# A graph kernel's gather buffers, handed out in pairs of quads instead of quad by quad

## The chip, the core and the metric

The kernel runs on one core of one Trainium2 chip. The metric is the device time of one execution in microseconds (us); where several executions were made, their median.

## What is computed

The reference is one message-passing layer of a graph network with a residual and a layer norm, in float32. There are N = 12500 nodes of D = 160 features (64 scalars and 32 vectors of 3) and E = 400000 edges, sorted by their destination `dst`.

```
h_s = s @ lin1_ws * a / sqrt(64);   h_v = v x lin1_wv * a / sqrt(32)        # per node
hid = silu(edge_scalars @ fc_w1 / 8);   w = hid @ fc_w2 / 8                  # per edge, 224 weights
es, ev = h_s[src], h_v[src]                                                  # a gathered row of 160 per edge
m_*   = products of the parts of w with es, ev and edge_attr (cross product included)
agg   = segment_sum(m_*, dst) / 4
o     = agg through lin2_ws, lin2_wv;   pre = sc + o;   gated = silu / sigmoid of pre
out   = layernorm(x + gated)
```

## The kernel before, in words

A first stage builds `h_tab`, the table of transformed nodes in DRAM (12500 rows of 160 floats, written by L350). It ends at about 60 us. All the rest is the edge stage, and the change lies in it.

**Tiles and quads.** A tile is 128 edges, one on each partition. There are 3125 tiles. `steps` (L131) groups them by four into 782 steps, here called quads 0 to 781 (the last has one tile). The loop at L814 walks through the quads. On each engine the instructions run in the order in which the loop writes them out (L807). Step n does this:

- `gather` (L450, called at L821): GpSimd issues one indirect DMA per tile (L454), four in a quad. Each fetches 128 rows of `h_tab`, chosen by the tile's `src`, into a quarter of a buffer `hg` of the pool `deep`, which has four such buffers (L656). Nothing else runs on GpSimd in this stage.
- `weights` (L467, TensorE): the 224 weights of every edge of the quad, into a PSUM buffer `pw`.
- `one_hot` (L530, VectorE): the edges' places in a window of 16 nodes, from `rel` and `iota`.
- `products` (L471, VectorE): one product at L477 and three at L485. They read `pw` and `hg` and write `pr`. The third L485 is the last reader of the quad's `hg`, and it is the one that raises VectorE's semaphore.
- `select_quad` (L539, VectorE): the one-hot rows times the edge attributes.
- `sum_up` for quad n-2 (L546, TensorE): the segment sums of the quad's four tiles, as matmuls into `pa`.
- In some steps more work is put in: `hidden` for every second quad (L445, L447), `close` (L735) and `turned` (L555 to L560) for finished blocks, `second` (L570, a burst of 22 matmuls) and `add` (L578), `finish` for finished nodes (L603 to L636), and `self_connection` (L715, L716).

**Waits.** An indirect gather waits on two things. It has one of eight DMA semaphores, used in turn, so it waits for the landing of the gather eight places before it. The first gather of a quad also waits on VectorE's semaphore, until the buffer's previous user is used up. With four buffers handed out in turn, the first gather of quad n waits for the third L485 of quad n-4. The first L477 of a quad waits for the landing of the quad's four gathers.

The loop at L885 redoes work for inputs whose destinations fall outside the windows; with these inputs its count is zero.

Of the kernel before, what the change touches and what calls it, by code (L numbers as in the profile page):

```python
# [10 lines left out]
F32 = mybir.dt.float32  # L11
# [9 lines left out]
P = 128  # L21
# [3 lines left out]
D = S + V3  # L25
# [6 lines left out]
Q = 4  # L32
# [21 lines left out]
def gnn_kernel(  # L54
# [104 lines left out]
    def index(t):  # L159
        a0, idx, _ = ahead(t)  # L160
        return idx[:, t - a0:t - a0 + 1]
# [62 lines left out]
    with tc.tile_pool(name="nodes", bufs=len(starts)) as nodes, tc.tile_pool(  # L224
        name="nodes_ps", bufs=6, space=PSUM
# [210 lines left out]
    def hidden(pool, psum, es, halves, t0, n):  # L436

        ph = psum.tile([2 * S, Q * P], F32, name="ph", tag="misc")
        hid = pool.tile([2 * S, Q * P], F32, name="hid")
        ends = [max(0, min(n, m - t0)) for m in halves]  # L440
        assert ends[0] >= ends[1]
        for k, c0, c1 in ((2 * S, 0, ends[1]), (S, ends[1], ends[0])):
            if c1 > c0:
                c = slice(c0 * P, c1 * P)
                nc.tensor.matmul(ph[:k, c], w1[:k, :k], es[:k, t0 * P + c0 * P:t0 * P + c1 * P],  # L445
                                 start=True, stop=True)
                nc.scalar.activation(hid[:k, c], ph[:k, c], AF.Silu, scale=1.0 / math.sqrt(64))  # L447
        return hid

    def gather(pool, idx):  # L450

        hg = pool.tile([P, Q, D], F32, name="hg")
        for t, i in enumerate(idx):
            nc.gpsimd.indirect_dma_start(  # L454
                out=hg[:, t, :], out_offset=None, in_=h_tab,
                in_offset=bass.IndirectOffsetOnAxis(ap=i, axis=0))
        return hg

    def weights(psum, hid, slots):

        pw = psum.tile([P, Q, 256], F32, name="pw")
        n = len(slots)
        for t in range(0, n, 2):
            half, c = slots[t]
            m = min(2, n - t)
            assert half == 0 and all(slots[t + k] == (k, c) for k in range(m))
            nc.tensor.matmul(pw[:, t:t + m, :NWT], hid[:m * S, c * P:(c + 1) * P], w2[:m * S, :m],  # L467
                             start=True, stop=True)
        return pw

    def products(pool, pw, hg, n, between=None):  # L471

        pr = pool.tile([P, Q, NPR], F32, name="pr", bufs=3)
        full = pr[:, :n, PIECE["w2a"] * V:]
        two = bass.AP(tensor=full.tensor, offset=full.offset,
                      ap=[full.ap[0], full.ap[1], [(PIECE["w1a"] - PIECE["w2a"]) * V, 2], [1, S]])
        nc.vector.tensor_mul(  # L477
            two,
            pw[:, :n, :2 * S].rearrange("p t (k c) -> p t k c", k=2),
            hg[:, :n, None, :S].to_broadcast([P, n, 2, S]))  # L480
        if between:
            between.pop(0)()
        for k, first in enumerate(("D0", "C0", "B0")):
            first = PIECE[first] * V
            nc.vector.tensor_mul(  # L485
                pr[:, :n, first:first + V3].rearrange("p t (i c) -> p t i c", i=3),
                pw[:, :n, None, 2 * S + k * V:2 * S + (k + 1) * V].to_broadcast([P, n, 3, V]),
                hg[:, :n, S:].rearrange("p t (i c) -> p t i c", i=3))
            if between:
                between.pop(0)()  # L490
        return pr
# [159 lines left out]
    with tc.tile_pool(  # L651
        name="fin", bufs=1
    ) as fin, tc.tile_pool(
        name="late", bufs=2
    ) as late, tc.tile_pool(name="edge", bufs=2) as edge, tc.tile_pool(
        name="deep", bufs=4  # L656
    ) as deep, tc.tile_pool(name="banks", bufs=1, space=PSUM) as banks:
        pw_ps = Banks(banks, "pw", Q * 256, 2)
        pa_ps = Banks(banks, "pa", 512, 2)
# [147 lines left out]
        with tc.manual_schedule(engines={ENG.PE, ENG.DVE, ENG.Activation, ENG.Pool}):  # L807
# [6 lines left out]
            for n, (c, i, tiles) in enumerate(steps):  # L814
# [6 lines left out]
                hg = gather(deep, [index(t) for t, _, _ in tiles])  # L821
# [63 lines left out]
        with tc.For_i(0, n_redo, 1):  # L885
            n_again = nc.values_load(again[0:1, 0:1], min_val=0, max_val=G)
            for half in range(2):
                nc.sync.dma_start(
                    bounds[:, :even].rearrange("o (c h k) -> o h c k", k=KB, h=2)[:, half],
                    in_pairs(rows[:, :even])[:, half])  # L890
            nc.sync.dma_start(bounds[:, even:], rows[:, even:])
            for t in range(BT):
                nc.sync.dma_start(of_tile[0].rearrange("(b t) -> b t", t=BT)[:, t:t + 1],
                                  bounds[0, :, None])
            with tc.For_i(0, n_again, 1) as g, tc.For_i(0, GT, 1) as k:
                t = g * GT + k
                idx = loads.tile([P, 1], I32, name="idx1", bufs=1)
                nc.sync.dma_start(idx, src[ds(g, 1), :, ds(k, 1)].rearrange("o p t -> p (o t)"))
                eat = loads.tile([P, 4], F32, name="eat1", bufs=1)
                nc.sync.dma_start(eat, ea[ds(g, 1), :, ds(k, 1)].rearrange("o p t k -> p (o t k)"))  # L900
                base0 = loads.tile([P, 1], I32, name="base1", bufs=1)
                nc.sync.dma_start(base0, of_tile[0:1, ds(t, 1)].to_broadcast([P, 1]))
                to = loads.tile([P, 1], I32, name="to1", bufs=1)
                nc.sync.dma_start(to, dst[:, ds(t, 1)])
                line = loads.tile([1, P], I32, name="line1", bufs=1)
                with nc.allow_non_contiguous_dma(reason="one tile's destinations"):
                    nc.sync.dma_start(line, dst[:, ds(t, 1)].rearrange("p o -> o p"))
                ends = loads.tile([1, 2], I32, name="ends1", bufs=1)
                for k, op in enumerate((OP.min, OP.max)):
                    nc.vector.tensor_reduce(ends[:, k:k + 1], line, AX.X, op)  # L910
                nc.sync.dma_start(least, ends[:, 0:1])
                low = loads.tile([P, 1], I32, name="low1", bufs=1)
                nc.sync.dma_start(low, least.to_broadcast([P, 1]))
                es = loads.tile([2 * S, SIDE * P], F32, name="es")
                nc.sync.dma_start(es[:S, :P], es_t[:, ds(t * P, P)])
                hid = hidden(edge, misc_ps, es, (1, 0), 0, 1)
                hg = gather(deep, [idx])
                pr = products(edge, weights(pw_ps, hid, [(0, 0)]), hg, 1)
                r = edge.tile([P, 1], F32, name="r", bufs=1)
                had = edge.tile([P, 2], F32, name="had", bufs=1)  # L920
                nc.vector.tensor_tensor(r, to, base0, op=OP.subtract)
                nc.vector.tensor_scalar(had[:, 0:1], r, 0.0, None, op0=OP.is_ge)
                nc.vector.tensor_scalar(had[:, 1:2], r, float(W), float(2 * NP), op0=OP.is_lt,
                                        op1=OP.mult)
                nc.vector.tensor_mul(had[:, 0:1], had[:, 0:1], had[:, 1:2])
                nc.vector.tensor_tensor(r, to, low, op=OP.subtract)
                nc.vector.tensor_add(r, r, had[:, 0:1])
                first = nc.values_load(ends[0:1, 0:1], min_val=0, max_val=N - 1)
                last = nc.values_load(ends[0:1, 1:2], min_val=0, max_val=N - 1)
                with tc.For_i(first, last + 1, W) as base:  # L930
                    base = nc.s_assert_within(
                        base, 0, N - 1, skip_runtime_bounds_check_because="it is at most `last`")
                    pa = pa_ps.tile([P, 512], F32, name="pa")
                    sel = select(late, r, eat)
                    add_tile(pa, 0, sel, 0, pr[:, 0], start=True, stop=True)
                    sa = late.tile([P, NPR], F32, name="sa")
                    nc.scalar.copy(sa[:ROWS], pa[:ROWS, :NPR])
                    tt = late.tile([P, 8, NO, W], F32, name="tt", bufs=1)
                    turned(misc_ps, sa, tt, 0, 1)
                    add(base, second(late, misc_ps, tt, 1), 0)  # L940
                    nc.vector.tensor_scalar_add(r, r, -float(W))
            for pool, job, most in [(fin, job, NF) for job in jobs] + [(fin, last_job, LAST)]:
                job_steps = finish(pool, misc_ps, *job, most=most)
                for f in job_steps[:job[1]]:
                    f()()
                for f in job_steps[job[1]:]:
                    f()
# [46 lines left out]
```

## Time and profile before

| what | value |
|---|---|
| median of 3 runs | 4008.95 us (4008.7 to 4012.74) |
| profiled execution, its own time | 4006.09 us |
| its span | 4004.3 us |
| mean granted TensorE clock | 0.968 |
| busy: TensorE / VectorE / ScalarE / GpSimd | 3666.2 / 2407.4 / 897.4 / 2973.4 us |
| the same as shares of the span | 92% / 60% / 22% / 74% |
| gathers L454: count, first and last start | 3125, 61.3 and 3971.1 us |

The profile is of one execution. [...] A group's line reads: line, engine, operation, out<-in, count | busy, mean ns of one | idle time of the engine just ahead of these instructions, and what ended most of it. "issue" means that the engine waited for nothing that the profile shows. The timeline lists instructions in order of time: start, duration, engine, line, and in brackets the idle time ahead. POOL is GpSimd, DVE is VectorE, ACT is ScalarE, PE is TensorE's matmuls and PEld its weight loads.

### The profile page before, as it was taken

The page shows a single profiled execution, that of the slowest core. Times are in us where ns is not written, and L with a number is a line of the kernel's source. Part 1 is how long each engine was busy: PE and PEld are TensorE (multiplying, and loading weights), DVE is VectorE, ACT ScalarE, POOL GpSimd, SP SyncE. Part 2 cuts the span into 40 slices and gives each one's busy share as a digit, 9 for nine tenths or more (in the row PEclk, how much of TensorE's full clock was granted, in tenths as well). Part 3 has the DMA queues.
Part 4 walks back from the last instruction along what each step waited for, and adds up shares of the span by engine and source line. Part 5 has one row for each costly group of instructions (what it writes and reads, how often), then busy time and mean ns, then how long its engine had stood idle before and what let it go on. Part 6 is the DMA issues. An engine that isn't in the chain of part 4 may idle for free. (4 is left out here: it accounts for less than half of the span.)

```text
span 4004.3 us, 46674 instructions
## 1 busy us (share of the span) xinstructions
PE 3666.2 (92%) x14291; PEld 1586.3 (40%) x14291; DVE 2407.4 (60%) x6508; ACT 897.4 (22%) x2488; POOL 2973.4 (74%) x3144
## 2 busy tenths in 40 slices
PE   6999899999989999999999899899898999989997
PEld 4344343443333433334334334344343433333343
DVE  5656565665665665656656556556565665665665
ACT  2222122221221221212212222122121221221222
POOL 4777777777777777777777777777777777777775
PEclk8999999999999999999999999999999999999998
DMA  8344344443443444444444444344344443443442
GB/s 243 95 100 101 95 106 98 105 101 95 105 102 95 106 102 95 103 99 101 102 99 102 98 103 104 95 106 102 95 106 98 104 100 95 109 99 96 102 98 54
DMA packets 227691, 411.71 MB, mean 103 GB/s; under 512 B 71883, under 2 KB 157383, under 8 KB 226535
## 3 DMA queue, kind: packets, MB, share of 16 engines
q0 software_dynamic: 152272, 266.53, 27.4%
q1 hardware_dynamic: 74646, 142.01, 14.6%
q8 instruction: 115, 1.88, 0.2%
q14 instruction: 144, 1.18, 0.1%
q10 hardware_dynamic: 514, 0.10, 0.0%
HBM read 392.41 MB, written 16.00 MB: 102 GB/s over the span
## 5 line engine op out<-in xcount | busy, mean ns | idle before, releaser
L454 POOL DMA_INDIRECT hg<-h_tab,idx x3125 | 2959.2, 947 | 958.2 <-issue 848.3
L467 PE MATMUL pw<-w,hid 128*128 128x448 f32 x3126 | 1370.6, 562 | 182.3 <-DVE sel L539 146.7
L546 PE MATMUL pa<-pr,sel 128*64 128x416 f32 x6250 | 1297.6, 537 | 0.0
L485 DVE TENSOR_TENSOR pr<-pw,hg 128x384 f32<-128x384 f32 x2346 | 1152.6, 546 | 0.0
L477 DVE TENSOR_TENSOR pr<-pw,hg 128x512 f32<-128x512 f32 x782 | 540.4, 691 | 992.3 <-DMA hg<-h_tab,idx 770.7
L467 PEld LDWEIGHTS pw<-w,hid 128*128 128x128 f32 x3126 | 555.9, 195 | 671.0 <-issue 453.2
L546 PEld LDWEIGHTS pa<-pr,sel 128*64 128x64 f32 x6250 | 386.2, 138 | 807.2 <-issue 797.1
L735 ACT COPY sa<-pa 128x416 f32<-128x416 f32 x521 | 263.2, 505 | 1259.4 <-PE pa L546 1257.2
L530 DVE TENSOR_TENSOR pw<-rel,iota 128x64 f32<-128x64 int16 x782 | 178.6, 228 | 500.6 <-PE pw L467 498.8
L445 PE MATMUL misc<-es,w 128*128 128x512 f32 (+1 forms) x784 | 452.7, 660 | 15.2 <-DMA es<-in_es_t_dram 13.5
L447 ACT ACTIVATE hid<-misc 128x512 f32<-128x512 f32 x392 | 233.5, 596 | 693.3 <-PE misc L445 693.0
L555 PEld LDWEIGHTS misc<-ident,sa 128*128 128x128 f32 x2084 | 240.3, 141 | 313.2 <-issue 265.6
L570 PE MATMUL misc<-tt,l 128*96 128x256 f32 (+5 forms) x1496 | 345.7, 378 | 4.6 <-DVE y L616 3.0
L555 PE MATMUL misc<-ident,sa 128*128 128x128 f32 x2084 | 328.6, 280 | 2.3 <-ACT hid L447 1.5
L539 DVE TENSOR_TENSOR sel<-pw,eas 128x256 f32<-128x256 f32 x782 | 321.8, 412 | 0.0
L570 PEld LDWEIGHTS misc<-tt,l 128*96 128x96 f32 (+1 forms) x1496 | 227.3, 163 | 143.3 <-issue 73.1
L558 ACT COPY tt<-misc 128x192 f32<-128x192 f32 x521 | 164.7, 316 | 505.5 <-PE misc L555 505.2
L445 PEld LDWEIGHTS misc<-es,w 128*128 128x128 f32 x784 | 120.1, 193 | 282.2 <-issue 224.7
L578 DVE TENSOR_TENSOR acc<-acc,os 96x32 f32 x1042 | 195.2, 187 | 25.2 <-ACT os L573 6.9
L603 PE MATMUL misc<-ident,acc 96*128 96x96 f32 x196 | 36.0, 269 | 95.4 <-DVE pw L530 46.2
L560 ACT COPY tt<-misc 128x64 f32<-128x64 f32 x521 | 117.1, 225 | 0.0
L573 ACT COPY os<-misc 96x512 f32<-96x512 f32 (+2 forms) x68 | 38.3, 563 | 296.4 <-PE misc L570 290.3
(83 smaller groups left out, 584.1 us busy)
## 6 DMA issues: line engine op xcount, KB each, us to landing
es<-in_es_t_dram SPq DMA_DIRECT2D x258, 384.0 KB
hg<-h_tab,idx POOLq DMA_INDIRECT x3125
h_tab<-ht POOLq DMA_DIRECT2D x6, 1280.0 KB
xt<-in_x_dram SPq DMA_DIRECT2D x23, 320.0 KB
out_dram<-y SPq DMA_DIRECT2D x23, 320.0 KB
xv<-in_xv_t_dram SPq DMA_DIRECT2D x25, 187.5 KB
xs<-in_xs_t_dram SPq DMA_DIRECT2D x25, 125.0 KB
xa<-in_xs_t_dram SPq DMA_DIRECT2D x6, 512.0 KB
```

The lines of the kernel that those rows point to most:

```text
L445: nc.tensor.matmul(ph[:k, c], w1[:k, :k], es[:k, t0 * P + c0 * P:t0 * P + c1 * P], start=True, stop=True)
L447: nc.scalar.activation(hid[:k, c], ph[:k, c], AF.Silu, scale=1.0 / math.sqrt(64))
L454: nc.gpsimd.indirect_dma_start(out=hg[:, t, :], out_offset=None, in_=h_tab, in_offset=bass.IndirectOffsetOnAxis(ap=i, axis=0))
L467: nc.tensor.matmul(pw[:, t:t + m, :NWT], hid[:m * S, c * P:(c + 1) * P], w2[:m * S, :m], start=True, stop=True)
L477: nc.vector.tensor_mul(two, pw[:, :n, :2 * S].rearrange("p t (k c) -> p t k c", k=2), hg[:, :n, None, :S].to_broadcast([P, n, 2, S]))
L485: nc.vector.tensor_mul(pr[:, :n, first:first + V3].rearrange("p t (i c) -> p t i c", i=3), pw[:, :n, None, 2 * S + k * V:2 * S + (k + 1) * ...
L539: nc.vector.tensor_mul(sel[:, :n], oh[:, :, None, :].to_broadcast([P, n, 4, W]), by_slot(tiles[0][0])[:, u:u + n, :, None].to_broadcast([P ...
L546: nc.tensor.matmul(pa[half * ROWS:(half + 1) * ROWS, :NPR], sel[:, t].rearrange("p k w -> p (k w)"), pr, start=start, stop=stop)
L555: nc.tensor.transpose(pt[:, four * P:four * P + k], sa[:k, c:c + P], ident[:k, :k])
L570: nc.tensor.matmul(po[:, k, :nb], l2[r, terms[to, part, four]], a[:, :nb], start=(n == 0), stop=(n == len(of) - 1))
L578: nc.vector.tensor_add(window, window, os[:, :, b])
L735: nc.scalar.copy(sa, pas.pop(j)[:, :NPR])
```

## The change

Instead of one buffer per quad, `gather` takes one tile of two quads from the pool and hands out its halves one after the other. The pool now has two such tiles, so the memory is the same: four quads of rows. A tile comes free as a whole. In the redo loop the list of halves is emptied ahead of the gather and after it.

```diff
+    pairs = []
+
     def gather(pool, idx):
 
-        hg = pool.tile([P, Q, D], F32, name="hg")
+        if not pairs:
+            both = pool.tile([P, 2, Q, D], F32, name="hg")
+            pairs.extend((both[:, 0], both[:, 1]))
+        hg = pairs.pop(0)
         for t, i in enumerate(idx):
             nc.gpsimd.indirect_dma_start(
...
-        name="deep", bufs=4
+        name="deep", bufs=2
...
+                pairs.clear()
                 hg = gather(deep, [idx])
+                pairs.clear()
```

In the instruction order of the two built programs, TensorE, VectorE, ScalarE and SyncE have the same instructions with waits on the same semaphores in the same places. On GpSimd the instructions are the same too; the waits on VectorE differ. Before, the first gather of every quad from quad 4 on has one. After, the first gather of every even quad from quad 4 on has one, and the odd quads have none. An even quad n opens the tile that held quads n-4 and n-3, so its wait is for the third L485 of quad n-3.

## The prediction

> **What bounds the kernel now.** I read the page's groups first, then the view of the tile `hg`, then the timeline of GpSimd and VectorE where they come closest. The groups:
>
> ```profile
> L454 POOL DMA_INDIRECT hg<-h_tab,idx x3125 | 2959.2, 947 | 958.2 <-issue 848.3
> ...
> L477 DVE TENSOR_TENSOR pr<-pw,hg 128x512 f32<-128x512 f32 x782 | 540.4, 691 | 992.3 <-DMA hg<-h_tab,idx 770.7
> ```
>
> GpSimd is busy 74%, TensorE 92%, so at first sight TensorE is the bound. The idle time says otherwise. GpSimd's 958.2 us over 3125 gathers is 0.307 us each, of which 848.3 us is "issue": a fixed gap behind every gather, not a wait. A gather takes 0.947 us and its gap 0.304, so one is issued each 1.251 us. The view of the tile has first and last start:
>
> ```profile
> L454 POOL DMA_INDIRECT hg<-h_tab,idx x3125: 942/946/1278, 61.3 to 3971.1; - x196
> ```
>
> 3124 x 1.251 = 3908 us, and 3971.1 - 61.3 = 3909.8. So **GpSimd's gathers run without one visible stall from end to end, and they bound the edge stage**. VectorE waits 770.7 us for their data. Before them lie 61 us of table building, behind them 3972.0 to 4004.3, the last sums and outputs. Any stall of GpSimd moves the end by as much, since nothing later catches up: TensorE and VectorE are ahead of their data and wait for it.
>
> **The change, step by step.** It adds and removes no instruction, no DMA and no byte: 3125 gathers as before, 4 quads of buffer as before. The order on PE, VectorE, ScalarE and SyncE is unchanged. What moves is one wait: the first gather of an even quad n waits for the third L485 of quad n-3 instead of n-4, and the odd quads' wait goes.
>
> *What the removed wait gives.* Nothing: it never holds. Over all quads from 4 on, the first gather starts 10.7 us (median) after the third L485 of quad n-4 ends, at the least 1.03 us (quad 4). Starts of first gathers of a quad follow their predecessor by 1.251 us, as the others do, so the wait costs no issue time either.
>
> *What the added wait costs.* I took from the timeline, for each of the 389 even quads from 4 to 780, the start of its first gather minus the end of the third L485 three quads earlier. This lead has a median of 5.5 us: GpSimd runs three quads (15.0 us) ahead, less 8.5 us from a quad's first gather to its last product. It is below 2 us in 33 places, below 1.03 in 16, below 0 in 6. The first is at the start, where VectorE still does setup when the gathers begin:
>
> ```profile
> 82.34 0.95 POOL L454 DMA_INDIRECT hg<-h_tab,idx  x1 [0.30 <-issue]
> ```
>
> ```profile
> 79.84 1.47 DVE L485 TENSOR_TENSOR pr<-pw,hg 128x384 f32<-128x384 f32 x3
> ...
> 82.43 1.47 DVE L485 TENSOR_TENSOR pr<-pw,hg 128x384 f32<-128x384 f32 x3
> ```
>
> The gather at 82.34 is the first of quad 4. It now waits for quad 0, done at 81.31; after the change for quad 1, done at 83.90: 1.57 us late. The largest one in the middle is quad 704:
>
> ```profile
> 3584.20 0.23 DVE L530 TENSOR_TENSOR pw<-rel,iota 128x64 f32<-128x64 int16 x1 [6.19 <-PE pw L467]
> 3584.47 0.69 DVE L477 TENSOR_TENSOR pr<-pw,hg 128x512 f32<-128x512 f32 x1
> 3585.08 1.47 DVE L485 TENSOR_TENSOR pr<-pw,hg 128x384 f32<-128x384 f32 x3
> ```
>
> ```profile
> 3584.43 0.94 POOL L454 DMA_INDIRECT hg<-h_tab,idx  x1 [0.30 <-issue]
> 3585.67 0.94 POOL L454 DMA_INDIRECT hg<-h_tab,idx  x1 [0.30 <-issue]
> ```
>
> VectorE sat idle for 6.19 us until TensorE gave it `pw`: TensorE did the burst of 22 matmuls of L570 and a slow stretch of L546 first. The products of quad 701 ended at 3586.55, the first gather of quad 704 started at 3585.67: 0.88 us late. Behind the waiting gather stand all later gathers, and the products wait for those.
>
> By place, the lateness (minus sign: lead left) is: quad 4 1.57, 32 -0.44, 128 0.08, 224 -0.25, 322 -0.35, 416 0.46, 476 0.00, 572 0.74, 608 -0.25, 704 0.88. Places close behind one of these (6 and 706, for example) are left out, as the stall gives them the same lead back. The rest have more than 0.87 left.
>
> *The price of a release.* A waiting gather doesn't start at the moment of the release; call the delay w. The trace shows no gather that waits for VectorE in earnest, so I bound it. Below: the six h_tab writes of L350 that wait for VectorE L339 start 0.29 to 0.31 us after its end, so w = 0.3. Above: quad 4's first gather started at its regular place with its release 1.03 us earlier, so w is at most 1.03. Nearest: the very first gather, the only one that found GpSimd idle, started at 61.27, after its last wait instruction ended at 60.47 (a record of the trace's semaphore events): w = 0.8. I take 0.8, as it is the same instruction; it may hold some start-up cost, which the range covers.
>
> The sum at w = 0.8: 2.37 + 0.36 + 0.88 + 0.55 + 0.45 + 1.26 + 0.80 + 1.54 + 0.55 + 1.68 = **10.4 us**. At w = 0.3 eight places are left and give 5.6 us; at w = 1.03 fourteen give 12.8. At w = 0 six give 3.7.
>
> [...]
>
> Against its own execution the sum is 4006.09 + 10.4 = 4016.5 us. The median of the runs shown is 2.9 us above that execution; the same 10.4 us on it give **4019.4 us**, which I forecast. No other cost: a stalled quad's data comes later, but VectorE is then behind by two quads whose data is there.
>
> **The rivals.**
>
> *Cheap release, no change that can be told (0.2%, 8.0 us, is about what a measurement of this kernel can tell).* If a blocked gather starts as promptly as the h_tab writes (w = 0.3), 5.6 us are left: 4014.5. The point from which it decides is w = 0.56, where the sum is 8.0. For it: six rows at 0.3, and the fixed gap between gathers is 0.304 too. Against: those are another kind of DMA, and the first gather took 0.8.
>
> *More stalls than this execution shows, slower.* Leads depend on when TensorE's bursts and late landings meet, which other executions may time otherwise. If every lead below 2 us became a stall at full price, the 33 places give up to 39 us (sum of 2 minus lead): 4048. For it: leads under 2 us are frequent. Against: the late places follow the written order, not chance: 32, 128, 224, 416, 608 and 704 lie multiples of 96 quads apart, and so do 476 and 572. I'd expect at most half, 4028.
>
> *The tile is tracked as a whole, so that the second quad of a pair waits for the products of the first.* Then GpSimd would stop at every odd quad for about 8.5 us minus 5.0, 390 x 3.5 = 1365 us: 5374. The instruction order has no wait on VectorE at odd quads, so this is nearly excluded.
>
> *Faster.* 389 waits go from GpSimd's order. If they cost anything, first gathers would follow later than the others; their mean distance is 1.2506 us against 1.2510 for the third of a quad. Nothing to win: 4009 at best.
>
> **How the numbers follow.** Forecast (w from 0.56 to 1.03, 4017 to 4022): 0.50. More stalls (4022 to 4048): 0.12. Cheap release, or stalls that other executions lack (4009 to 4017): 0.33. Whole-tile tracking: 0.01. Faster by over 0.2%: 0.04, for a cause that I don't see. So faster 0.04, same 0.33, slower 0.63. The range takes in the forecast, the lower end w = 0.3 (4014.5) less 2 us for fewer stalls, and half of the dense case: 4012.5 to 4028.
>
> **What would show it.** Right: GpSimd's groups keep 947 ns a gather, and its idle time grows by some 10 us, which the waits view puts on VectorE, L485 above all, in about ten places, quad 4 first with over 2 us; the last gather starts about 10 us later; VectorE's wait for gathers grows alike. Wrong if the gathers still run at 1.251 us throughout (the wait never bites), if the stalls sit at places with leads over 2 us, if a stall is much longer than its lateness plus 1 us, or if the mean gather or its gap changes.

## The result, and the profile after

The changed kernel takes **4017.59 us** in the median of 20 runs (4012.94 to 4028.3); the kernel before takes 4012.35 us in 20 runs beside it (4007.69 to 4020.15). The ratio is 1.0014, 95% interval 1.0008 to 1.0020, or 3 to 8 us. So the change costs some 5 us: clear of zero, and under the 0.2% (8 us) that the prediction called a difference.

The profiled execution has a span of 4020.5 us, 16.2 more than that of before. Most of this isn't the change. The view of the tile `hg` gives first and last start of the gathers (L459 is the old L454; from `gather` on, line numbers are 5 higher):

```profile
L459 POOL DMA_INDIRECT hg<-h_tab,idx x3125: 942/946/2334, 68.2 to 3985.2; - x196
```

The first gather starts 7.0 us later than in the profile of before. It waits for the whole of `h_tab`, and by the trace's semaphore events the last rows, which SyncE writes (L353), landed at 67.3 us instead of 60.3. Another profile of the same changed kernel starts at 61.3 (experiment 5). After the last gather 35.3 us follow instead of 33.2. Between first and last gather lie 3917.0 us instead of 3909.8: these 7.2 us are the part to explain. The page's groups:

```profile
L459 POOL DMA_INDIRECT hg<-h_tab,idx x3125 | 2961.0, 948 | 970.7 <-issue 901.8
...
L482 DVE TENSOR_TENSOR pr<-pw,hg 128x512 f32<-128x512 f32 x782 | 540.4, 691 | 1013.6 <-DMA hg<-h_tab,idx 808.5
```

A gather still takes 0.947 us and its gap 0.305. The gathers' own time is 1.8 us more; it differs by as much between executions (experiment 5 has 2958.5). VectorE's wait for gathers (808.5 instead of 770.7) differs between executions too: it is 762.1 in experiment 5, so it tells nothing of the change. The rest are waits. The view of GpSimd's waits (total, times, longest) now has VectorE's products with gaps over 0.3:

```profile
POOL hg L459 <- issue: 901.8, 2960, 0.3
...
POOL hg L459 <- DVE pr L490: 8.8, 12, 1.6
```

Of these 12, four are the usual gap, only named after VectorE. Eight are stalls; without the usual gap they are 0.87, 0.28, 0.79, 1.12, 0.03, 1.27, 0.16 and 0.64 us, **5.2 us in all**, at quads 92, 320, 322, 380, 382, 476, 572 and 704. All are first gathers of even quads. The longest is quad 476. The timeline of GpSimd there:

```profile
2455.03 0.95 POOL L459 DMA_INDIRECT hg<-h_tab,idx  x1 [0.30 <-issue]
2457.55 0.94 POOL L459 DMA_INDIRECT hg<-h_tab,idx  x1 [1.57 <-DVE pr L490]
2458.80 0.95 POOL L459 DMA_INDIRECT hg<-h_tab,idx  x1 [0.30 <-issue]
```

And of VectorE, which was using up quads 472 and 473:

```profile
2441.09 0.69 DVE L482 TENSOR_TENSOR pr<-pw,hg 128x512 f32<-128x512 f32 x1 [4.32 <-DMA hg<-h_tab,idx]
...
2453.78 0.26 DVE L535 TENSOR_TENSOR pw<-rel,iota 128x64 f32<-128x64 int16 x1 [5.98 <-PE pw L472]
...
2455.80 1.48 DVE L490 TENSOR_TENSOR pr<-pw,hg 128x384 f32<-128x384 f32 x3
```

Quad 473's last product ends at 2457.28 and the gather starts at 2457.55: **0.27 us after its release**. At all eight stalls the two starts and ends give 0.27.

Quad 476 also shows what lies ahead of a late product. TensorE's timeline and, below it, the busy times in three stretches (the column behind the five engines is TensorE's granted clock):

```profile
2438.64 1.67 PE L472 MATMUL pw<-w,hid 128*128 128x448 f32 x4
2442.78 0.55 PE L608 MATMUL misc<-ident,acc 96*128 96x96 f32 x2 [2.47 <-DVE y L621]
2443.26 2.83 PE L551 MATMUL pa<-pr,sel 128*64 128x416 f32 x8
2446.03 1.13 PE L445 MATMUL misc<-es,w 128*128 128x512 f32 x2
2446.99 5.25 PE L575 MATMUL misc<-tt,l 128*96 128x256 f32 x22
2452.08 1.67 PE L472 MATMUL pw<-w,hid 128*128 128x448 f32 x4
```

```profile
2432.00:2442.00 10.00, 7.67 (x32) 3.21 (x28) 4.30 (x12) 2.31 (x7) 7.56 (x9) 1.00 0.67 145
2442.00:2447.00 5.00, 4.22 (x13) 1.52 (x14) 4.86 (x14) 0.85 (x2) 3.78 (x5) 0.66 0.27 66
2447.00:2457.00 10.00, 10.00 (x44) 5.85 (x43) 3.65 (x11) 1.96 (x5) 6.84 (x8) 1.00 0.28 68
```

Read it from the top, as an order in time; that each step causes the next is not shown by it. A chunk of edge data is loaded (DMA share 0.67), a gather lands late, and VectorE waits 4.32 us for it. TensorE waits for VectorE and sits idle for 2.47 us. Towards the end of this its clock is halved for 3.4 us (by the trace's clock records from 2442.3 to 2445.8), and the eight L551 take 2.83 us instead of 1.62. The burst of 22 matmuls L575 follows, 5.25 us, and only behind it the weights `pw` that quad 473's products need. Each of the eight stalls has such a burst, or the end of one, in the 16 us ahead of it; of all even quads in this trace, 37% have one. Five of the eight have a half-clock stretch in the 18 us ahead; of all even quads, 22% have one.

### The profile page after: what moved, and what is told of

The parts are those of the page before. It is cut to its first block, busy times and chain, and to the rows that moved or that the text cites. A ratio compares the mean times of both kernels' runs of the same rounds, so it can differ in the third digit from the quotient of the medians.

```text
span 4020.5 us, 46285 instructions
## 1 busy us (share of the span) xinstructions
PE 3668.3 (91%) x14291; PEld 1584.5 (39%) x14291; DVE 2406.6 (60%) x6508; ACT 898.6 (22%) x2488; POOL 2975.3 (74%) x3144
## 5 line engine op out<-in xcount | busy, mean ns | idle before, releaser
L459 POOL DMA_INDIRECT hg<-h_tab,idx x3125 | 2961.0, 948 | 970.7 <-issue 901.8
L551 PE MATMUL pa<-pr,sel 128*64 128x416 f32 x6250 | 1300.4, 538 | 0.0
L482 DVE TENSOR_TENSOR pr<-pw,hg 128x512 f32<-128x512 f32 x782 | 540.4, 691 | 1013.6 <-DMA hg<-h_tab,idx 808.5
L551 PEld LDWEIGHTS pa<-pr,sel 128*64 128x64 f32 x6250 | 387.3, 139 | 811.1 <-issue 801.3
L535 DVE TENSOR_TENSOR pw<-rel,iota 128x64 f32<-128x64 int16 x782 | 178.8, 229 | 495.2 <-PE pw L472 493.2
L575 PE MATMUL misc<-tt,l 128*96 128x256 f32 (+5 forms) x1496 | 345.6, 378 | 7.6 <-DVE y L621 5.5
L575 PEld LDWEIGHTS misc<-tt,l 128*96 128x96 f32 (+1 forms) x1496 | 227.0, 162 | 144.6 <-issue 73.0
```

What stands on the lines that cost most here:

```text
L459: nc.gpsimd.indirect_dma_start(out=hg[:, t, :], out_offset=None, in_=h_tab, in_offset=bass.IndirectOffsetOnAxis(ap=i, axis=0))
L482: nc.vector.tensor_mul(two, pw[:, :n, :2 * S].rearrange("p t (k c) -> p t k c", k=2), hg[:, :n, None, :S].to_broadcast([P, n, 2, S]))
L551: nc.tensor.matmul(pa[half * ROWS:(half + 1) * ROWS, :NPR], sel[:, t].rearrange("p k w -> p (k w)"), pr, start=start, stop=stop)
L575: nc.tensor.matmul(po[:, k, :nb], l2[r, terms[to, part, four]], a[:, :nb], start=(n == 0), stop=(n == len(of) - 1))
```

## The experiments

**State of the theories.** *Stall theory*: the change costs the late places at pair openings, each its lateness plus a release price, and nothing else. *Pairing rival*: handing out in pairs costs something besides. Open beside these: what the price is, and what makes products late.

The first four kernels ran on another chip than the others, and there the kernel before took 5190.29 us instead of about 4010. I tell them after their repetitions.

**1. The change itself again** (experiment 5; no edit).

> The changed kernel itself, beside the kernel before. Where TensorE is granted a clock of about 0.97 (before near 4010 us), the stall theory has about eight stalls on VectorE L490, 4 to 7 us together, each starting 0.27 us after the release, and a ratio of 1.001 to 1.002; the quads that stall need not be the same ones. Where TensorE is granted about 0.87 (before near 5190 us, as on the chip of the first four experiments), gathers wait hundreds of times, and the pairing rival has the change 2% slower, since the moved pairs were 2.1% slower there; the stall theory in its first form, in which only the lead of three quads counts, has it like three single buffers, which were 0.4% faster there.

Measured: 4019.84 against 4015.74 us, ratio 1.0005 (0.9996 to 1.0014). The interval holds the first measurement's 1.0014, and also 1, no change. Its profile is clearer than its times. GpSimd's waits:

```profile
POOL hg L459 <- DVE pr L490: 8.1, 12, 2.8
```

There are seven stalls, 4.5 us in all: quad 4 with 2.53, and 128, 380, 382, 476, 572 and 704 with 0.02 to 0.78, each 0.27 us after its release. From first to last gather it is 3913.6 us. So quad 4 stalls when the gathers start early (61.3 us), and not when they start at 68.2; 380, 476, 572 and 704 come in both.

**2. More room: three tiles of two quads** (experiments 1 and 6).

```diff
-        name="deep", bufs=2
+        name="deep", bufs=3
```

> The change with three tiles of two quads again. At a clock of about 0.97: stall theory no gather waits for VectorE, ratio 1.000 within 0.001; pairing rival 1.0013. At about 0.87: 1.03 again, as in the first run of it.

Measured: 4015.48 against 4015.74 us, ratio 0.9997 (0.9988 to 1.0006). The view of GpSimd's waits has four entries for VectorE's products, all of them the usual gap:

```profile
POOL hg L459 <- DVE pr L490: 1.2, 4, 0.3
```

No stall; first to last gather 3909.7 us, as before (3909.8). Pairs as such cost nothing that can be told on this chip. The expectation for the same kernel on the other chip is told below.

**3. The pairs moved by one quad** (experiments 2 and 7).

```diff
             hide(0)
+            pairs.append(deep.tile([P, Q, D], F32, name="hg0", bufs=1))
```

> The pairs moved by one quad again. At a clock of about 0.97: stall theory at most two stalls near the start, up to 1 us, ratio 1.000 within 0.001; pairing rival 1.0013. At about 0.87: 1.02 again.

Measured: 4015.94 us, ratio 1.0001 (0.9992 to 1.0010). Two stalls, 0.33 us at quad 323 and 0.87 us at quad 609, 1.2 us in all; first to last gather 3910.6 us. The amount is as expected and the places aren't (not near the start). The output burst is always written into a step of the same parity, and the products behind it, of odd quads, are what an even quad's opening waits for. One quad further, a pair opens on the products behind those, and these are late less often: in the trace of before, eight even quads have a lead of under 0.27 us over the last product three quads back, and two odd ones (5 and 23).

**4. Three single buffers** (experiments 3 and 8): on the kernel before, `bufs=4` becomes `bufs=3`.

> Three buffers of one quad again. At a clock of about 0.97: stall theory the same stalls as the change and at most 1 us more, 4 to 7 us, ratio 1.001 to 1.002; pairing rival 1.000. At about 0.87: 0.996 again.

Measured: 4019.64 us, ratio 1.0008 (0.9999 to 1.0017), beside the change's 4019.84 in the same job. Five stalls, 5.4 us: quad 3 with 3.59 at the start, 23, 92, 476 and 704. So a lead of three quads stalls about as much with no pairs in it. The time alone doesn't show that: from first to last gather it is 3923.0 us, since a gather took 949 ns instead of 947, here and in experiment 3, which is 7 us over all of them. The reason is open.

**5. The same memory handed out in one piece** (experiment 10): tiles of four quads, one of them.

```diff
-            both = pool.tile([P, 2, Q, D], F32, name="hg")
-            pairs.extend((both[:, 0], both[:, 1]))
+            both = pool.tile([P, 4, Q, D], F32, name="hg")
+            pairs.extend(both[:, k] for k in range(4))
...
-        name="deep", bufs=2
+        name="deep", bufs=1
```

> The same memory handed out still more coarsely: one tile of four quads, whose first gather waits until all four are used up (the products of the quad just before). Stall theory: every fourth quad stalls, 195 stalls; a quad's products end 8.5 us after its first gather starts and the next quad would start 5.0 us after it, so each costs 3.5 + 0.27 us at least and more where products are late; by the trace of before 970 us, ratio 1.24 at a clock of 0.97. With a release price of 0.8 it would be 1070 us. If TensorE were the bound instead of GpSimd, the stalls would be covered and the ratio far smaller.

Measured: 4983.53 against 4008.80 us, ratio 1.2427 (1.2408 to 1.2446), 975 us more where 970 were expected. All 195 openings stall, 983 us together. Of GpSimd's timeline, one opening:

```profile
2007.14 0.95 POOL L459 DMA_INDIRECT hg<-h_tab,idx  x1 [0.30 <-DMA hg<-h_tab,idx]
2008.39 0.97 POOL L459 DMA_INDIRECT hg<-h_tab,idx  x1 [0.30 <-issue]
2014.77 0.94 POOL L459 DMA_INDIRECT hg<-h_tab,idx  x1 [5.41 <-DVE pr L490]
2016.02 0.95 POOL L459 DMA_INDIRECT hg<-h_tab,idx  x1 [0.30 <-issue]
```

191 of the stalled gathers start 0.27 us after the release and four 1.74 us after it. Stalls of GpSimd go nearly one to one into the time here: 983 us of stalls, 975 us of time. A plain sum over the leads in the trace of before, with 0.27 us for each release, gives 1040 us, so the leads size these stalls to some 6%.

**6. Two single buffers** (experiment 11): on the kernel before, `bufs=4` becomes `bufs=2`.

> The kernel before with two buffers of one quad: every quad waits for the products two quads earlier, half the memory. Stall theory: from the leads in the trace of before some 145 stalls, 230 us together, ratio 1.057 at a clock of 0.97, each stalled gather 0.27 us after its release. With a price of 0.8 it would be 295 us. If the change's cost came from the pairing and not from the lead, this kernel would be no slower than before by its stalls alone.

Measured: 4291.35 us, ratio 1.0696 (1.0680 to 1.0712), 283 us more. There are 202 stalls, 288 us together, more than the 145 and 230 expected, though 190 of them start 0.27 us after the release (12 after 1.74). The total lies near the one worked out with a price of 0.8, but that isn't its reason. The leads of before don't size this kernel well: where each stall moves all later gathers and products along, they give 223 stalls and 412 us, more than measured. TensorE idles more here (88% busy instead of 92%) and its granted clock is 0.952 instead of 0.968, so products are late at other places; how much that adds is not shown.

**7. The price that was put too high** (experiment 9): one more gather ahead of the first.

```diff
     nc.gpsimd.dma_start(dt, dst)
+    warm = consts.tile([P, D], F32, name="warm")
+    nc.gpsimd.indirect_dma_start(
+        out=warm, out_offset=None, in_=x,
+        in_offset=bass.IndirectOffsetOnAxis(ap=index(0), axis=0))
```

> The change with one more indirect gather, of 128 rows of x into a tile that nothing reads, on GpSimd ahead of the first gather of h_tab. It asks why the release price was put at 0.8 us: the first gather starts 0.80 us after its last wait instruction in every profile, a stalled gather 0.27 us after the product that releases it. If 0.8 is a cost of the first indirect gather of a program, the first gather of h_tab now starts about 0.3 us or less after its last wait instruction and the extra one takes the 0.8; if it belongs to a wait instruction ahead of any gather on an idle GpSimd, it stays at 0.8.

Measured, by GpSimd's timeline (in this kernel the gather is at L463):

```profile
56.31 1.04 POOL L359 DMA_INDIRECT warm<-in_x_dram,idx  x1 [0.30 <-issue]
62.15 0.97 POOL L463 DMA_INDIRECT hg<-h_tab,idx  x1 [4.80 <-DMA h_tab<-ht]
```

The last of the separate wait instructions ahead of the gather at 62.15 ended at 61.43 (by the trace's semaphore events), so it started 0.72 us behind it instead of 0.80. A first-time cost is at most 0.08 of it, and the 0.1 us by which the first gather is longer (1.04) moves to the extra one. Where the other 0.72 comes from is not shown. The first gather differs from a stalled one in two ways: it stands behind separate wait instructions, and all that it waits for are landings of DMAs, while a stalled gather carries its last wait itself, and that wait is for VectorE. No run here has one without the other.

The kernel's time in its one run was 4012.98 us, which tells nothing by itself. But its trace is a third profile of the change: nine first gathers stall, 4.4 us in all, at quads 4, 32, 188, 224, 322, 476, 572, 608 and 668, each 0.27 us after its release.

**8. Shorter bursts** (experiments 4 and 12): on the change, `NO = 16` becomes `NO = 8`.

> The change with NO = 8 again, bursts of half the columns twice as often. At a clock of about 0.97: stall theory fewer than three stalls on L490, under 1.5 us in all, not counting quad 4 at the start; TensorE's busy time grows by 50 to 100 us within its idle 330 us; ratio 0.999 to 1.001. Rival (late landings make products late): the same seven or eight stalls. A third way: more work on TensorE makes more products late and the stalls grow. At about 0.87: 1.02 again.

Measured: 4012.16 against 4008.80 us, ratio 1.0008 (0.9998 to 1.0017). There are nine stalls, 3.8 us in all, not fewer than three and under 1.5. On the page the bursts have 128 columns, and VectorE's products are still waited for (the next line is from the view of waits):

```profile
L575 PE MATMUL misc<-tt,l 128*96 128x128 f32 (+2 forms) x2926 | 385.7, 279 | 1.5 <-ACT tt L565 1.5
```

```profile
POOL hg L459 <- DVE pr L490: 5.9, 10, 1.0
```

The length of one burst isn't what decides. The stalls sit at other quads (56, 152, 442, 536, 698, 728 and so on), and seven of the nine have a half-clock stretch in the 18 us ahead, where 27% of the even quads have one. No quad 4 is among them (the gathers started at 65.5). My account of a burst as the cause was too simple: late products seem to need several things together, and a half-clock stretch is often among them. What makes products late stays open.

**9. The first four, on a chip where TensorE's granted clock was lower** (experiments 1 to 4). The expectations, in the order of the kernels above, three pairs, moved pairs, three singles, short bursts:

> The change with a third tile of two quads (six quads of rows instead of four), so the first gather of an even quad n waits for the products of quad n-5. Stall theory (the change costs only the late places at pair openings, each its lateness plus 0.27 us): no gather waits for VectorE, the idle time of the gathers falls by 5 us against the changed kernel, and the time is that of the kernel before, ratio 1.000 within 0.001. Rival (handing out in pairs costs something else: the start, longer gathers, a sequencer that runs less far ahead): still about 5 us slower than before, ratio 1.0013. If the release price were 0.8 us, the result here would be the same as by the stall theory.

> The change with the pairs moved by one quad: quad 0 has a buffer of its own, pairs are quads 1 and 2, 3 and 4, and so on, so that odd quads open the pairs and wait for the products three quads earlier. Stall theory: the late products are those of odd quads, behind a burst of 22 matmuls that is always written into a step of the same parity, and an odd quad waits for an even one. From the trace of before, two odd quads (5 and 23) have leads under 0.27 us, 1.0 us together, from the trace of the change none: 0 to 1 us of stalls, ratio 1.000 within 0.001. Rival (any pairing costs): 5 us, ratio 1.0013.

> The kernel before with three buffers of one quad instead of four: every quad waits for the products three quads earlier, the even ones as in the change. Stall theory: the change's stalls and at most 1 us more, 5 to 6 us, ratio 1.0013 to 1.0015, with the stalled quads almost all even. Rival (the cost lies in the pairing, not in the lead of three quads): as before, ratio 1.000.

> The change with NO = 8 instead of 16: the output step L575 comes twice as often, with 22 matmuls of half the columns. Stall theory: the burst of some 5 us gets shorter, so products behind it are less late; fewer than three stalls on VectorE L490, under 1.5 us in all, although TensorE gets more to do (some 60 more bursts; its busy time may grow by 50 to 100 us). The time goes back to about that of before, ratio 0.999 to 1.001, if TensorE's idle time covers its extra work. Rival (late products come from late landings of gathers, not from TensorE's burst): the same eight or so stalls, 5 us, or more.

Measured, against 5190.29 us before: three pairs 5367.46 (ratio 1.0315, 1.0284 to 1.0346), moved pairs 5305.22 (1.0211, 1.0178 to 1.0243), three singles 5167.19 (0.9961, 0.9936 to 0.9986), short bursts 5299.86 (1.0195, 1.0160 to 1.0230). Every expectation missed. The page of three pairs:

```profile
PEclk7888888888888888888888888888888888888898
...
L459 POOL DMA_INDIRECT hg<-h_tab,idx x3125 | 2956.2, 946 | 2312.3 <-DVE pr L490 1358.0
...
L535 DVE TENSOR_TENSOR pw<-rel,iota 128x64 f32<-128x64 int16 x782 | 182.7, 234 | 2638.1 <-remote 1231.1
```

TensorE's mean clock is 0.861 there (28% of the time at half), and VectorE is idle for 2638 us ahead of L535: 790 us of it ended by TensorE's `pw`, 1231 by something that the profile can't name. GpSimd, now no bound, waits 1358 us for VectorE even with six quads of room. So the stall theory's first condition, that the gathers bound the stage, is false on that chip, and its numbers don't apply. Whether the low clock is the cause is not shown: in experiment 10, on a chip that showed 0.97 with the kernel before, stalls left TensorE busy for 80% of the span instead of 92%, and the clock was 0.897. So a low clock goes with idle time there, and which comes first can't be told. There the three kernels that pair were 2 to 3% slower and three singles a little faster. The change itself wasn't run there. Why more room makes that chip slower is **open**.

## Why the prediction was right or wrong

*The gathers bound the stage: right on the chips of the result.* With no stall (three pairs) the time is that of before, and 983 us of stalls make 975 us of time. It was wrong on the chip of experiments 1 to 4, where the clock was 0.86.

*The removed wait gives nothing: right.* Three pairs have no effective wait on VectorE at all, and a ratio of 0.9997.

*The added wait bites at a few even quads, by the leads of before: right in kind and number.* Ten places were listed; eight stalls came in the first profile and seven in the second. Quads 322, 476, 572 and 704 (first) and 4, 128, 476, 572 and 704 (second) were on the list; 92, 320, 380 and 382 weren't, with leads over 0.9 us in the trace of before. In the first profile the listed places give 2.9 of the 5.2 us, and quad 4, which was to stall most, doesn't stall; in the second they give 4.3 of 4.5, in that of experiment 9 3.4 of 4.4. So the total agrees better than the places do, and in the first profile that is partly luck. The places recur at distances of 96 quads, as was said, but which of them are late differs by execution. Half-clock stretches are often near (five of the eight stalls in the first profile have one in the 18 us ahead). Of the 48 such stretches in the trace of before, 26 last 3.4 us and 20 last 6.8; in the 3.4 us ahead of one TensorE was idle for 2.7 us in the median. Why the places change from execution to execution is not shown by any run here.

*The price of a release: the step that failed.* The prediction bounded it by 0.3 and 1.03 and took 0.8, "the same instruction", from the first gather. It is 0.27 (all but a few, told below). The row that looked nearest was of the same instruction but of another wait (separate instructions, for landings), and its 0.8 doesn't carry over. The `h_tab` writes, the prediction's lower bound, are another operation, but they carry a wait for VectorE as a stalled gather does, and their 0.29 to 0.31 was close. With 0.27 the prediction's own list keeps eight places, 1.84 + 0.35 + 0.02 + 0.73 + 0.27 + 1.01 + 0.02 + 1.15 = 5.4 us, against 5.2 and 4.5 us of stalls in the two profiles and 5.2 us between the medians. The term was 10.4 us, twice too large. Nor is 1.03 a bound for every release: some took 1.74 us (experiments 10 to 12), though no first gather of a quad in the three profiles of the change. So the rival of the cheap release came, and the difference stays under 8 us, where "slower" had the larger chance.

*A length that was misread.* The prediction puts 8.5 us between a quad's first gather and its last product. That is near the shortest in the trace of before (8.4 us); the median is 9.4, which fits the median lead of 5.5 us (15.0 less 8.5 would be 6.5). The sum by places doesn't use it; the 1365 us of the whole-tile rival does, and is too small by it.

*The time.* 4019.4 was forecast and 4017.59 measured, and that they are only 1.8 us apart is luck: the term was some 5 us too large, and the median of before, 4012.35 over 20 runs, is 3.4 us above the one that I added to.

*More stalls than one execution shows: didn't come.* The sum stays at 4.4 to 5.2 us in the three profiles, although the places change.

## What to carry to other kernels

A buffer pool on a bounding engine can be priced by its leads: for each hand-out, when the engine wants the buffer minus when the last reader is done. Here this gave 5.4 us for the change against 5.2 and 4.5 measured, 1040 against 983 for one tile of four quads, but 412 against 288 for two singles. On the chips of the result, four quads of room in singles leave at least 1 us and cost nothing; in pairs they lead by three quads and cost 5 us; in one piece they cost 975 us. When you price a wait that no trace shows, look for a row that waits in the same way (for the same engine, the wait carried by the instruction itself), before one of the same operation: here the `h_tab` writes with 0.3 us, not the first gather with 0.8.

## What the runs showed of the hardware

- A gather that is held back by VectorE's semaphore starts 0.27 us after the releasing product ends (in 191 of 195 cases of experiment 10).
- In 18 cases of experiments 10 to 12 it is 1.74 us, and these aren't scattered: all are first gathers of quads 6 + 53 k (112, 165, 218, 271 and so on), 212 gathers or a multiple of it apart. From quad 112 on, no gather that waits for VectorE at such a place starts sooner than 1.74 us after its release in any profile here, while the stalled gathers elsewhere in these three experiments all start 0.27 us after it. With one gather more ahead (experiment 9) the place moves: there the second gathers of quads 32 and 668, 12 times 53 quads apart, start 0.27 us late. The cause is open. In experiment 12 one such release fell while the gather ahead was still being issued, 0.87 us ahead of the regular start, and still cost 0.88 us.
- GpSimd took one wait far ahead of use: in the trace of before, the wait of the 17th gather for an earlier landing was over 7.7 us before that gather started, with six others between.
- The same kernel took 4012 us on one chip and 5190 us on another, with a granted TensorE clock of 0.97 and 0.87, and the order of four variants was another there. Whether the longer time follows from the lower clock is not shown.
